# Strassen products for the linear maps of a two-layer graph attention kernel, with their weights' combinations streamed from DRAM

## The chip, the cores and the metric

The kernel runs on one core of a Trainium2 chip. The metric is the device time of one launch in microseconds (us); quoted times are medians of four runs or more, with the lowest and highest beside them (e7_ring6 was run once). The profile shows one execution. In it PE is TensorE (matmul), PEld its weight load, DVE is VectorE, ACT is ScalarE, POOL is GpSimd, and SP issues DMAs; L341 is line 341 of the kernel that the profile belongs to.

## The reference, cut to what matters

```python
# x: (32, 512, 512) float32, adj: (512, 512) int32 of 0 and 1, all weights 512 x 512 float32
def layer0(x):
    mi, mj = x @ Wi.T, x @ Wj.T                  # Wi, Wj: the halves of W (512, 1024)
    a = adj.astype(float32); deg = a.sum(axis=1)
    return deg[None, :, None] * (mi + b) + einsum('ij,bjo->bio', a, mj)

def layer1(h):                                   # 8 heads of 64
    q, k, v = h @ Wq.T + bq, h @ Wk.T + bk, h @ Wv.T + bv
    scores = where(adj == 0, -inf, q k^T / 8)    # by head
    return softmax(scores) v @ Wo.T + bo

x = layernorm(x + layer0(x))
x = layernorm(x + layer1(x))
```

Everything is float32. For one of the 32 batches there are six maps of a 512x512 activation by a 512x512 weight (two of layer 0, then V, Q, K and the output map), beside scores, values, row sums and one aggregation with the adjacency.

## The kernel before: the parts that the change touches

The kernel gives TensorE its work in one order. For batch `b` there are eight steps; each puts two blocks of scores, the values of the step before and, every second step, the row sums ahead of a share of the linear maps of the neighbouring batches. Every map works in 512-column matmuls from resident weights, with two PSUM banks `mm` taken in turn.

```python
def mm_tile():
    return psum.tile([P, 512], FT, name="mm", bufs=2)

def l0_out(b, ic):                               # layer 0, 128 rows of the result
    y = XT[b][:, ic, :]
    nc.vector.scalar_tensor_tensor(y, b0_r, deg_c[:, ic:ic + 1], y, op0=OP.mult, op1=OP.add)
    pm = mm_tile()
    for w, src in ((0, XD[b]), (1, AX_T[b])):
        for dc in range(DC):
            nc.tensor.matmul(pm, src[:, dc, ic * P:(ic + 1) * P], (wi, wj)[w][:, dc, :], ...)
    ...
    nc.vector.tensor_add(y, y, pm)

def q_out(b, hp):                                # ScalarE evicts Q and K
    pm = mm_tile()
    for dc in range(DC):
        nc.tensor.matmul(pm, wq[:, dc, hp * P:(hp + 1) * P], HT[b][:, dc, :], ...)
    nc.scalar.activation(QT[b, hp], pm, AF.Identity, bias=bq_c[:, hp:hp + 1], scale=QSCALE)

def scores(b, hp, kc): ...                       # PE scores, ACT exp, DVE mask product and sum
def invert(b, hp, part): ...                     # reciprocal of the row sums, in halves
def scale(b, hp):
    pl, rl = RL[hp]
    nc.vector.tensor_tensor_reduce(t, pl, rl, 1.0, 0.0, OP.add, OP.add, told[:, j:j + 1])
    OT[b, hp] = work([P, N], "oT", 6)
    nc.vector.tensor_mul(OT[b, hp], PV[hp], rl)  # the scaled head pair, input of the output map

for step in range(STEPS):                        # of a batch; cut
    scores(b, hp, 2 * half); scores(b, hp, 2 * half + 1)
    values(...)                                  # of the step before
    ...
    while at < len(todo) and done < total * (step + 1) / STEPS - 1e-6:
        while extra and todo[at][1] is proj:     # what is left of invert and scale goes first
            g = extra.pop(0); g[0](*g[1:])
        run(todo[at]); done += todo[at][0]; at += 1
        if extra:                                # else one of them after each piece
            g = extra.pop(0); g[0](*g[1:])
```

## Time and profile before

| | before |
|---|---|
| time | 4171.16 us (4170.17 to 4171.29) |
| profiled span, mean granted TensorE clock | 4170.1 us, 0.997 |
| TensorE busy | 4129.6 us, 99% |
| one batch in mid-run ("period") | 128.49 us, no TensorE idle |
| first scores of batch 1 start | 105.8 us |
| first period, which has no output map yet | 113.97 us |
| tail, after the 31st period | 95.5 us |

The page's lines and the rows that this table rests on stand in the prediction. A span is read here as start, then 31 periods from the first scores of batch 1 (each period ends at the first scores of the next of the 32 batches), then the tail after the last of them. A row of "stretches" gives the length of a stretch and then the busy time of PE, weight load, DVE, ACT and POOL, the granted clock, the share of the DMA engines and GB/s.

### The profile page before, as it was taken

To read this page: it belongs to the slowest core of one execution; us is meant where nothing else is said; L and a number is where in the kernel's file an instruction comes from. 1 tells how busy PE (TensorE), PEld (TensorE's weight loads), DVE (VectorE), ACT (ScalarE), POOL (GpSimd) and SP (SyncE) were. 2 spreads that over 40 slices of the span, in tenths; PEclk is the share of its full clock that TensorE was granted. 3 is DMA by queue.
4 is the path that set the end of the run, shared out by engine and by line. 5 is a ranking of instruction groups with operands and counts; after the bars stand their busy time and mean duration, and the time that the engine had idled before them with its cause. 6 is when DMAs were issued, how large, how long until landed. Compare 5 with 4: busy or idle time off the path is not lost.

```text
span 4170.1 us, 31849 instructions
## 1 busy us (share of the span) xinstructions
PE 4129.6 (99%) x12826; PEld 1784.0 (43%) x12826; DVE 2554.7 (61%) x2953; ACT 891.2 (21%) x1159; POOL 566.2 (14%) x782
## 2 busy tenths in 40 slices
PE   8999999999999999999999999999999999999997
PEld 4444444444444444444444444444444444444442
DVE  2566656666557665566565666655766556656567
ACT  1212221222221222212222122221222221222211
POOL 1111111111111111111111111111111111111111
PEclk9999999999999999999999999999999999999999
DMA  3000000000000000000000000000000000000000
GB/s 108 1 21 21 5 16 20 21 20 21 1 20 21 21 21 0 21 21 21 21 0 21 20 21 21 14 7 21 21 21 21 0 21 21 21 21 1 21 10 21
DMA packets 37945, 77.34 MB, mean 19 GB/s; under 512 B 1248, under 2 KB 1248, under 8 KB 37792
## 3 DMA queue, kind: packets, MB, share of 16 engines
q1 hardware_dynamic: 35376, 70.26, 4.7%
q10 hardware_dynamic: 2112, 4.19, 0.3%
q8 instruction: 103, 1.69, 0.2%
q0 software_dynamic: 304, 0.79, 0.1%
q14 instruction: 50, 0.41, 0.0%
HBM read 41.68 MB, written 33.55 MB: 18 GB/s over the span
## 4 chain that ended last, share of the span: by engine, by line
PE 98%; DVE 2%; DMA 0%; ACT 0%; POOL 0%; issue 0%
PE mm L223 21%; PE sc L276 11%; PE ov L293 11%; PE mm L265 11%; PE mm L249 11%; PE mm L257 11%; PE mm L321 11%; PE mm L206 6%; PE ov L300 3%; PE sc L239 2%; PE sc L199 1%; DVE e L280 0%; DVE rl L306 0%; DMA l<-in_adj_dram 0%; DVE es L285 0%; DVE es L283 0%
## 5 line engine op out<-in xcount | busy, mean ns | idle before, releaser
L280 DVE TENSOR_TENSOR e<-e,edge 128x1024 f32<-128x1024 f32 x512 | 710.6, 1408 | 957.0 <-ACT e L279 956.9
L279 ACT ACTIVATE e<-sc 128x1024 f32<-128x1024 f32 x512 | 496.3, 1021 | 1519.3 <-PE sc L276 1519.3
L276 PE MATMUL sc<-q,k 64*128 64x512 f32 x2048 | 510.6, 617 | 0.0
L293 PE MATMUL ov<-e,v 128*64 128x512 f32 x2048 | 496.9, 605 | 6.2 <-DVE e L280 3.7
L265 PE MATMUL mm<-l,wk 128*128 128x512 f32 x1024 | 466.7, 598 | 0.0
L321 PE MATMUL mm<-wo,oT 128*128 128x512 f32 x1024 | 460.0, 602 | 5.6 <-DVE oT L314 5.6
L223 PE MATMUL mm<-wi,l 128*128 128x512 f32 x1024 | 460.6, 592 | 0.0
L257 PE MATMUL mm<-l,wq 128*128 128x512 f32 x1024 | 460.4, 592 | 0.0
L223 PE MATMUL mm<-wj,l 128*128 128x512 f32 x1024 | 460.3, 592 | 0.0
L249 PE MATMUL mm<-wv,l 128*128 128x512 f32 x1024 | 450.3, 592 | 0.0
L306 DVE RECIPROCAL rl<-ov 128x256 f32<-128x256 f32 x256 | 438.2, 1733 | 0.0
L187 POOL TENSOR_TENSOR xlo<-xh,xhi 128x512 fp32r<-128x512 f32 x128 | 165.5, 1301 | 1512.5 <-ACT xhi L186 1512.5
L285 DVE TENSOR_TENSOR es<-es,e 128x1024 f32<-128x1024 f32 x256 | 313.5, 1225 | 8.8
L321 PEld LDWEIGHTS mm<-wo,oT 128*128 128x128 f32 x1024 | 189.8, 190 | 274.0 <-issue 218.0
L276 PEld LDWEIGHTS sc<-q,k 64*128 64x128 f32 x2048 | 176.7, 186 | 304.0 <-issue 293.0
L265 PEld LDWEIGHTS mm<-l,wk 128*128 128x128 f32 x1024 | 189.5, 190 | 265.2 <-issue 215.7
L257 PEld LDWEIGHTS mm<-l,wq 128*128 128x128 f32 x1024 | 194.5, 190 | 245.2 <-issue 245.2
L223 PEld LDWEIGHTS mm<-wj,l 128*128 128x128 f32 x1024 | 194.6, 190 | 244.9 <-issue 244.9
L173 POOL TENSOR_SCALAR mv<-mv 128x1 f32<-128x1 f32 x256 | 71.0, 278 | 1660.4 <-DVE mv L172 1660.4
L227 DVE TENSOR_TENSOR xh<-xh,mm 128x512 f32<-128x512 f32 x128 | 88.0, 688 | 319.0 <-PE mm L223 319.0
L249 PEld LDWEIGHTS mm<-wv,l 128*128 128x128 f32 x1024 | 189.5, 190 | 214.6 <-issue 214.6
L223 PEld LDWEIGHTS mm<-wi,l 128*128 128x128 f32 x1024 | 189.5, 190 | 213.8 <-issue 211.3
(62 smaller groups left out, 2891.7 us busy)
## 6 DMA issues: line engine op xcount, KB each, us to landing
xh<-in_x_dram SPq DMA_DIRECT2D x32, 1024.0 KB, 5.1
out_dram<-xh SPq DMA_DIRECT2D x32, 1024.0 KB, 4.3
wj<-in_wjT_dram ACTq DMA_DIRECT2D x1, 1024.0 KB, 11.9
l<-in_adj_dram SPq DMA_DIRECT2D x1, 1024.0 KB, 9.7
wi<-in_wiT_dram ACTq DMA_DIRECT2D x1, 1024.0 KB, 16.8
wv<-in_wvT_dram SPq DMA_DIRECT2D x1, 1024.0 KB, 20.5
wk<-in_wkT_dram ACTq DMA_DIRECT2D x1, 1024.0 KB, 21.6
wq<-in_wqT_dram SPq DMA_DIRECT2D x1, 1024.0 KB, 25.4
```

The lines of the kernel that those rows point to most:

```text
L206: nc.tensor.matmul(pm, parts[w][:, jc, :], adjR[:, jc, :], start=(w == 0 and jc == 0), stop=(w == 1 and jc == NC - 1))
L223: nc.tensor.matmul(pm, src[:, dc, ic * P:(ic + 1) * P], (wi, wj)[w][:, dc, :], start=(w == 0 and dc == 0), stop=(w == 1 and dc == DC - 1))
L249: nc.tensor.matmul(pm, HT[b][:, dc, ic * P:(ic + 1) * P], wv[:, dc, :], start=(dc == 0), stop=(dc == DC - 1))
L257: nc.tensor.matmul(pm, wq[:, dc, hp * P:(hp + 1) * P], HT[b][:, dc, :], start=(dc == 0), stop=(dc == DC - 1))
L265: nc.tensor.matmul(pm, wk[:, dc, hp * P:(hp + 1) * P], HT[b][:, dc, :], start=(dc == 0), stop=(dc == DC - 1))
L276: nc.tensor.matmul(ps[:, s, :], KT[b, hp][r, kc * P:(kc + 1) * P], QT[b, hp][r, :], start=True, stop=True)
L279: nc.scalar.activation(e, ps, AF.Exp)
L280: nc.vector.tensor_tensor(e, e, edge[:, kc:kc + 1, :].to_broadcast([P, 2, N]), op=OP.mult)
L285: nc.vector.tensor_add(ES[hp], ES[hp], e)
L293: nc.tensor.matmul(PV[hp][s * HD:(s + 1) * HD, :], V[b][:, kc, c0:c0 + HD], E[kc][:, s, :], start=(kc == 0), stop=(kc == NC - 1))
L306: nc.vector.reciprocal(rl[:, c], pl[:, c])
L321: nc.tensor.matmul(pm, OT[b, hp][:, ic * P:(ic + 1) * P], wo[:, hp, :], start=(hp == 0), stop=(hp == HP - 1))
```

## The change

Strassen's scheme (in Winograd's form) makes a 512x512x512 product from seven products of 256x256x256 instead of eight. The intent is to take up to an eighth of the linear maps' time off TensorE, which is the bound (busy for 99% of the span, and 98% of the chain that ended last). The price is additions: of the weights' quarters once, of the activations' quarters for every batch (on POOL), and of the products (on VectorE and POOL). The weights' tiles, seven for each of six maps, are not kept in SBUF: they are written to DRAM at the start and read back for every batch into a ring of 12 tiles. Two maps run at a time, piece by piece in turn, each with one PSUM bank, and pieces that share a result are accumulated in that bank between evictions.

The diff, cut to its core (the cut parts are the fallback path, the start and the small steps of the norm):

```diff
-    def mm_tile():
-        return psum.tile([P, 512], FT, name="mm", bufs=2)
+    def mm_tile(bank):
+        return psum.tile([P, 512], FT, name="mm" + bank, bufs=1)
...
+    RING = 12
+    def combine(name, eng):                      # once per weight
+        a11, a12, a21, a22 = ...
+        eng.tensor_tensor(s1, a21, a22, op=OP.add)        # s2, s3, s4 alike
+        for i, t in ((1, a11), (2, a12), (6, s2), (7, s3), (4, n22), (5, s1), (3, s4)):
+            WS[name, i] = dram.tile([P, 2, Q], FT, ...)
+            nc.sync.dma_start(WS[name, i], t)
+    def prefetch():                              # keeps RING tiles ahead of TensorE
+        while len(TILES) < min(len(KEYS), ring.used + RING):
+            t = ring_tile()
+            nc.sync.dma_start(t, WS[KEYS[len(TILES)]])
...
+    def base(b):                                 # was in l0_out, one 128-row block at a time
+        for ic in range(NC):
+            nc.vector.scalar_tensor_tensor(y, b0_r, deg_c[:, ic:ic + 1], y, ...)
+    def combos(T, b, quarters, which, part=None):  # activations' combinations
+        for i in which:
+            dst, p, q = {1: (t1, b12, b11), 2: (t2, b22, t1), 3: (t3, b22, b12), 4: (t4, t2, b21)}[i]
+            nc.gpsimd.tensor_tensor(dst, p, q, op=OP.subtract)
+    GROUP = {1: "X", 2: "X", 6: "Y", 7: "Y", 4: "Y", 5: "Z", 3: "Z"}
+    def piece(kind, b, i, bank):                 # one of the seven products, 8 or 16 records
+        if first: OPEN[kind, b, g] = mm_tile(bank)
+        ...
+                    nc.tensor.matmul(pm[:, c * Q:(c + 1) * Q], lhs, rhs, start=first, ...)
+        prefetch()
+        if i == 1: nc.scalar.copy(p1, pm)        # product 1 is wanted in every quarter
+        if kind in ("l0", "pj"):                 # layer 0 and the output map add into x
+            if i == 1: three nc.gpsimd.tensor_tensor(d, d, p1, op=OP.add)
+            else:      nc.vector.tensor_tensor(d, d, pm, op=OP.add)
+        elif kind == "v": ...                    # nc.scalar.copy or nc.vector.tensor_tensor
+        else: ...                                # Q and K: two activations for piece 2,
+                                                 # else two nc.vector.scalar_tensor_tensor
...
+    ORDER = (1, 2, 6, 7, 4, 5, 3)
+    def phase_a(n):   # K pieces of n-1 in bank a, between the aggregation of n
+        ...
+            res += k[i:i + 1] + g[i:i + 1]
+            if i == 1 and g:
+                res += [z(combos, TX, n, ..., (1,)), z(combos, TA, n, ..., (1,))]
+        if g: res += [..., z(base, n), ...]
+    def project(m, i):
+        res = [pc("pj", m, i, "b")]
+        if i == 2:
+            res = [FLUSH] + res + [z(combos, TO, m, ot_quarter(m), (2, 3, 4))]
+    def phase_b(n):   # layer 0 of n in bank a, output map of n-2 in bank b, in turn
+        for i in ORDER:
+            res.append(pc("l0", n, i, "a"))
+            ...
+            res += project(m, i)
+    def phase_c(n):   # V in bank a, Q in bank b, the first K pieces
+        res = [norm[0], norm[1], z(apply, n, 1), z(add_bo, n, 0), pc("v", n, 1, "a")]
+        ...
+        res += [pc("q", n, 1, "b"), pc("v", n, 2, "a"), pc("q", n, 2, "b")]
+        ...
+        res += [norm[2], z(combos, TH, n, h, (1, 2), 0), pc("k", n, 1, "a"), norm[3], ...,
+                z(combos, TH, n, h, (3, 4), 1), z(add_bo, n, 1), pc("k", n, 2, "a")]
+        for i in ORDER[2:]:
+            res += [pc("v", n, i, "a"), pc("q", n, i, "b")]
...
-                while extra and todo[at][1] is proj: ...
+                if todo[at] is FLUSH:            # only here the rest of invert and scale goes first
+                    while extra: ...
```

## The prediction

> **What bounds the kernel now.** I read the page's engine shares and chain first, then stretches of one period, then the groups with their shapes, then narrow timelines. In the page's first and fourth parts:
>
> ```profile
> PE 4129.6 (99%) x12826; PEld 1784.0 (43%) x12826; DVE 2554.7 (61%) x2953; ACT 891.2 (21%) x1159; POOL 566.2 (14%) x782
> ...
> PE 98%; DVE 2%; DMA 0%; ACT 0%; POOL 0%; issue 0%
> PE mm L223 21%; PE sc L276 11%; PE ov L293 11%; PE mm L265 11%; PE mm L249 11%; PE mm L257 11%; PE mm L321 11%; PE mm L206 6%; PE ov L300 3%; PE sc L239 2%; PE sc L199 1%; DVE e L280 0%; DVE rl L306 0%; DMA l<-in_adj_dram 0%; DVE es L285 0%
> ```
>
> TensorE is both the busiest engine and the path. The linear maps (L223, L265, L249, L257, L321) are 65% of it. A stretch of one batch in mid-run (columns: length, then busy time of PE, weight load, DVE, ACT, POOL; clock):
>
> ```profile
> 1027.40:1155.89 128.49, 128.49 (x402) 55.50 (x401) 79.59 (x93) 27.66 (x36) 17.36 (x24) 1.00 0.05 17
> ```
>
> A period is 128.49 us with no TensorE hole. The first scores start at 105.83 us; 31 periods bring it to 4089; the tail to 4170 is 81. So time = start + 31 periods + tail.
>
> The pace of one matmul, in the timeline of PE and in the groups:
>
> ```profile
> 2011.73 3.60 PE L257 MATMUL mm<-l,wq 128*128 128x512 f32 x8
> 2015.17 3.60 PE L265 MATMUL mm<-l,wk 128*128 128x512 f32 x8
> ```
>
> The second starts 3.44 us after the first: 8 records, 4 matmuls, so 0.43 us a record (two records a float32 matmul). The groups' mean of 592 ns includes the pipeline's latency and is not the pace.
>
> [...] the trace shows 188 to 190 with latency, which would hide under 216 only just. The last matmul of the kernel settles it:
>
> ```profile
> L410 PE MATMUL mm<-tot,ones 128*128 128x1 f32 x2 | 0.4, 260 | 3.9 <-DVE tot L408 3.9
> L410 PEld LDWEIGHTS mm<-tot,ones 128*128 128x128 f32 x2 | 0.3, 188 | 4.7 <-DVE tot L408 4.7
> ```
>
> Two loads of 188 ns cover only about 0.3 us and two matmuls of 260 ns about 0.4, so a load-and-multiply pair can repeat every 0.13 us or so: loads do not set the pace at 216. [...]
>
> ```profile
> 2135.14 1.23 DVE L280 TENSOR_TENSOR e<-e,edge 128x1024 f32<-128x1024 f32 x1 [10.34 <-ACT e L279]
> ...
> 2149.96 3.33 DVE L280 TENSOR_TENSOR e<-e,edge 128x1024 f32<-128x1024 f32 x2 [9.95 <-ACT e L279]
> 2148.56 2.51 POOL L187 TENSOR_TENSOR xlo<-xh,xhi 128x512 fp32r<-128x512 f32 x2 [43.07 <-ACT xhi L186]
> ```
>
> The mask product costs 1.23 us alone; two take 3.33 rather than 2.4 where POOL was in its subtraction. [...] In the tail, where TensorE stood idle, the stretches show it (seventh number of a row is the clock):
>
> ```profile
> 4081.50:4084.90 3.40, 0.57 (x2) 0.00 (x0) 3.37 (x5) 0.00 (x0) 0.00 (x0) 0.98 0.00 0
> 4084.90:4091.70 6.80, 6.59 (x14) 2.02 (x16) 3.09 (x6) 1.78 (x2) 0.74 (x2) 0.51 0.01 2
> ```
>
> **The change part by part.**
> TensorE, removed: 6 maps x 16 matmuls x 2 records x 429 ns = 82.4 us a period. Added: 6 maps x 7 products x 4 matmuls x 2 records x 216 ns = 72.6. The other 46.1 us (scores, values, sums, transposes, aggregation) stay. Floor of a period: 118.7 us, 9.8 less. A full eighth of 82.4 would be 10.3[...].
>
> VectorE: before 79.6 us a period. Added, with a 128x512 add from PSUM at 0.69 (row L227): two more evictions each for layer 0 and the output map, one for V, and for Q and K, which ACT evicted, two adds and six half-size adds each (about 0.4). That is 5 x 0.69 + 2 x (1.4 + 2.4) = 11 us. Reciprocals are cut in four, about 0.6 more in all. Some 91 to 92 us, 77% of the floor: not the bound on average.
>
> POOL: before 17.4. Added: 16 combinations and 6 adds of 128x512 at 1.3 (row L187): 29 us, so 46[...].
>
> DMA: 42 tiles of 256 KB, 11 MB a period, 93 GB/s, plus x and the output. At the start this trace moved 385 GB/s, and the ring looks 12 tiles, some 20 us, ahead. Hidden.
>
> What is not hidden is order. Each of two PSUM banks now belongs to one piece of 1.73 us, so an eviction must be through before the other bank's piece ends; before, it had 3.4 us or more. I walked one period in the instruction order of the changed kernel, which has eight steps (scores, values, then pieces), with this trace's durations (VectorE operations that do not depend on one another start 0.08 us early):
> - Step 1. The second output piece needs the last head pair's scaled output. VectorE has two reciprocal quarters, the accumulating pass (0.69) and the scaling (0.69) in its queue behind the eviction of the layer-0 piece just before. From the end of that piece: 0.2 signal + 0.6 eviction + 0.83 + 0.94 (quarters, half of the 1.73 of row L306) + 0.62 + 0.69 + 0.1, less the 0.43 of a first matmul that need not wait: **3.5 us** of TensorE idle.
> - Step 4. VectorE arrives 3.0 us late (reciprocal, pass and scaling of the pair before), then has two mask products and two sums (4.8), statistics (1.7) and the eviction of the last output piece (0.7) ahead of the first Q piece: it can start at 10.2 us into the step, and would have at 8.1. **2.0 us**.
> - Step 5: V's third piece waits for a POOL combination made after the transposes, 0.6. Step 6: an eviction behind two products and two sums, 0.6.
> - [...] (POOL's adds against sums in step 4, its combinations against products in step 8): about 1.0, the weakest number[...].
> Sum 7.7 us, so a period of 126.4.
>
> Start: all weights must be combined, 42 tiles stored and read back before the first piece, since stores and ring loads share one queue in order. 9 MB in and 11 MB out at 385 GB/s is 52 us; first piece at about 55 where before it was 35; then layer 0 alone 24, Q, K, V 36, gathers and norms 11, waits 8: first scores at about 135 (before 105.8, but one batch's gather, 9.3, has moved into it from the periods). Tail about 6 longer. Fixed part 135 - 9 + 87 = 213.
>
> Time = 213 + 31 x 126.4 = 4131; I choose 4125.
>
> **Rivals.** (a) The pure TensorE count wins: the walk is too pessimistic, VectorE catches up, no hole: 213 + 31 x 119 = 3900. For it: TensorE bound at 99%, VectorE at 77%. Against: the hole in step 1 is a fixed chain, not a matter of load. With holes of some 4 us: 4013.
> (b) [...]a hole of 3.5 us leaves a window of 3.4 us mostly empty, and in the tail of this trace a window at 0.57 of 3.40 busy was followed by 6.8 us at half clock. If most periods pay 1.7 to 3.4 us: 4190 to 4220.
> (c) [...]with 24 products and normalizations a period each blocked 1 us, VectorE would be near 110 us busy and the period about 130: 4240.
> (d) The ring starves: only if a store of x blocks the queue for over 20 us; a 1 MB store lands in 4.3 here. Unlikely.
>
> **Range and chances.** (a) half true and (b) or (c) half true bound the range: 3990 to 4250. 4088 is the 2% line, which is a period of 125.0, only 1.4 us below my own, and the walk's terms are each uncertain by as much; a hand walk also tends to count holes that overlap. So faster 0.35, same 0.45, slower 0.20.
>
> **What would show each step.** Pieces of 8 records spaced 1.73 us: the floor is right. PE waits on DVE at the output map's pieces totalling about 110 us (31 x 3.5), and at the Q pieces about 60: the walk is right. DVE busy near 92 to 96 us a period, POOL near 46 to 50; mask products' mean far over 1.4 us would speak for (c); a clock below 1.00 in mid-run stretches for (b); PE waits on DMA in mid-run for (d). I would be wrong low if the narrow matmul's pace is above 216 ns, and wrong high if the output pieces do not wait.

The paces in its count can be read in the traces: from the start of one record of a linear map to the start of the next it is mostly 429 ns at 512 columns in the kernel before and 216 ns at 256 columns in the changed kernel. When the count was made no trace had a record of 256 columns, and its 216 was the estimate; half of the 0.43 us of the trace is 0.215. The half clock after a window that TensorE left mostly idle, and the longer products beside POOL's work, stand in the rows that it prints: a clock of 0.51 after 0.57 us busy of 3.40, and 3.33 us for two products of 1.23 us each. The 188 to 190 ns there are the profile's time of one weight load. By what means POOL's work makes VectorE's longer, no trace shows.

## The result, and the profile after

| | before | after |
|---|---|---|
| time | 4171.16 us (4170.17 to 4171.29) | 4300.54 us (4299.13 to 4303.21) |
| profiled span, mean granted clock | 4170.1 us, 0.997 | 4297.4 us, 0.971 |
| first scores of batch 1 | 105.8 us | 141.3 us |
| first period, no output map yet | 113.97 us | 110.27 us |
| period in mid-run, mean of the second to the 30th | 128.49 us | 131.44 us |
| mean of the first 30 periods | 128.01 us | 130.73 us |
| last period | 128.49 us | 124.3 us |
| tail | 95.5 us | 109.8 us |

Two of these stretches of the kernel before, its first period and its tail:

```profile
105.83:219.80 113.97, 112.39 (x357) 48.58 (x357) 65.82 (x71) 27.66 (x36) 13.90 (x16) 1.00 0.00 1
...
4074.58:4170.07 95.49, 72.21 (x223) 24.19 (x222) 72.43 (x88) 16.30 (x17) 11.97 (x16) 0.91 0.06 23
```

The kernel is slower: the ratio of after to before is 1.0311, with a 95% interval of 1.0294 to 1.0329. A ratio is the mean time of one kernel's runs over that of the other's in the same rounds, so it is not quite the ratio of the two medians. The result is numerically correct, as are all the experiments below.

First the page of the changed kernel: the busy times, then the chain that ended last, by engine.

```profile
PE 3967.8 (92%) x17442; PEld 2710.3 (63%) x17442; DVE 3057.1 (71%) x3898; ACT 878.9 (20%) x1230; POOL 1628.2 (38%) x1626
...
PE 71%; DVE 22%; ACT 3%; POOL 2%; issue 1%; SPq 0%; DMA 0%; ACTq 0%; DVEq 0%; POOLq 0%
```

TensorE lost 162 us of busy time and yet the span grew by 127: it is busy for 92% where it was 99%, and the chain now runs through VectorE for 22% where it was 2%. The two kinds of work take turns in waiting for each other.

The 30 periods as one stretch of the changed kernel:

```profile
141.27:4063.27 3922.00, 3681.12 (x16254) 2518.69 (x16253) 2834.17 (x3605) 812.51 (x1139) 1493.93 (x1486) 0.98 0.33 100
```

By 30, a period has 122.70 us of TensorE busy and 8.03 us idle (without the short first period, 123.30 and 8.13); VectorE is busy for 94.5 us, POOL for 49.8. The idle part is in a few rows of PE's waits (the columns are us in total, times, and the longest):

```profile
PE mmb L341 <- DVE oT L437: 103.0, 30, 3.4
PE mma L341 <- DVE k L384: 62.4, 31, 2.1
PE mma L341 <- POOL big L310: 29.3, 30, 1.0
PE ov L414 <- DVE told L432: 28.0, 36, 3.0
...
PE mmb L341 <- DVE xh L359: 12.3, 29, 0.4
...
PE mma L341 <- ACT p L348: 9.8, 31, 0.3
PE mma L341 <- ACT big L287: 7.4, 31, 0.2
```

The number of times, about 30, says that each is a fixed place of the period, not chance. The biggest is the second piece of the output map (bank b, `mmb`) behind the last scaled head pair `oT`. It looks like this in the changed kernel's timelines of PE and of DVE (start, length, engine, line, and in brackets the idle time before and its releaser):

```profile
1970.58 3.62 PE L341 MATMUL mma<-ring,big 128*128 128x256 f32 x16
1974.04 0.59 PE L341 MATMUL mmb<-ring,oT 128*128 128x256 f32 x2
1978.07 2.93 PE L341 MATMUL mmb<-ring,oT 128*128 128x256 f32 x6 [3.43 <-DVE oT L437]
...
1974.31 0.69 DVE L359 TENSOR_TENSOR xh<-xh,mma 128x512 f32<-128x512 f32 x1 [0.29 <-PE mma L341]
1974.91 1.76 DVE L427 RECIPROCAL rl<-ov 128x128 f32<-128x128 f32 x2
...
1977.32 0.69 DVE L437 TENSOR_TENSOR oT<-ov,rl 128x512 f32<-128x512 f32 x1
```

This is the hole that the prediction walked: VectorE evicts the layer-0 piece that ended at 1974.0, and only then finishes the reciprocals, the pass and the scaling. VectorE is not late for that eviction: it waited 0.29 us for TensorE before it. Earlier in its queue lie four base additions, which took 6.30 us from 1961.55.

The six matmuls after the hole take 2.93 us where six at the pace of full clock take 1.5 (an estimate from the pieces below: 6 x 0.216, and 0.16 for the end of the last). Stretches of one window each around that hole and around the second largest wait (first number after the comma: PE busy; seventh: the clock):

```profile
1973.62:1977.03 3.41, 1.01 (x5) 0.56 (x3) 3.08 (x5) 0.00 (x0) 3.41 (x3) 1.00 0.47 154
1977.03:1983.86 6.83, 5.79 (x14) 4.63 (x15) 1.67 (x4) 0.00 (x0) 6.21 (x6) 0.50 0.14 41
2082.84:2086.25 3.41, 1.45 (x7) 0.82 (x5) 3.38 (x5) 0.58 (x1) 0.35 (x1) 1.00 0.24 77
2086.25:2089.66 3.41, 3.29 (x8) 2.66 (x9) 0.67 (x2) 0.00 (x0) 0.00 (x0) 0.50 0.00 0
```

After 3.41 us with TensorE busy for 1.01 the clock is halved for 6.83 us; after a window with 1.45 it is halved for 3.41 us. The clock records of this run hold full and half clock alone, so its mean clock of 0.971 makes 2 x 0.029 x 4297 = 249 us at half clock.

In the clock records of the changed kernel and of the one before, all changes of a run lie on one grid of 3.413 us. Cutting the 30 periods of the changed kernel along it gives 1097 windows at full clock and 51 at half. The 37 of the 1097 that were followed by half clock had TensorE busy, by the profile's count, for 1.49 us or less; the other 1060 had 1.52 or more. Of the 51 at half clock, 37 had at least 2.91 us busy and were followed by full clock; the other 14 had at most 2.38 and were followed by half clock again. This is what these windows show and no rule: in the tail of the kernel before, a window with 3.05 us busy was followed by half clock. In these periods, then, a hole was followed by half clock where it left some 1.9 us (3.41 - 1.49) or more of one window idle, and where the grid fell decided whether it did.

The changed kernel shows what this costs without any edit. Its periods drift against the grid, and two of them, three periods apart, read:

```profile
909.34:1042.63 133.29, 125.16 (x546) 85.72 (x545) 94.92 (x121) 27.10 (x38) 50.17 (x51) 0.96 0.34 99
...
1304.76:1435.00 130.24, 122.11 (x545) 83.58 (x544) 94.93 (x121) 27.10 (x38) 50.16 (x51) 0.99 0.34 101
```

Both have 8.13 us of idle TensorE and the same work, but 10.24 and 3.41 us at half clock, three windows and one: the difference is 3.05 us in TensorE's busy time. In mid-run a period has 6.00 us at half clock on average.

The second wait, in step 8, in the timelines of DVE, POOL and PE:

```profile
2078.43 3.62 DVE L397 TENSOR_TENSOR e<-e,edge 128x1024 f32<-128x1024 f32 x2 [1.12 <-ACT e L396]
2081.97 3.56 DVE L406 TENSOR_TENSOR es<-es,e 128x1024 f32<-128x1024 f32 x2
2085.45 0.87 DVE L384 SCALAR_TENSOR_TENSOR k<-mma,bk_c,p 128x256 f32<-128x256 f32 x2
...
2078.71 4.48 POOL L310 TENSOR_TENSOR big<-big 128x512 f32<-128x512 f32 x2
...
2086.37 3.60 PE L341 MATMUL mma<-big,ring 128*128 128x256 f32 x8 [2.08 <-DVE k L384]
```

VectorE's two products and two sums run beside POOL's two combinations and are long by about 1.1 us for each pair (3.62 and 3.56 us, where e4_combos_dve has 2.54 and 2.47 without them); the eviction of K's piece behind them is late by that, and the next K piece uses the same bank.

At full clock and without a wait, the pieces run as follows:

```profile
2056.30 1.89 PE L341 MATMUL mma<-ring,big 128*128 128x256 f32 x8
2058.03 1.89 PE L341 MATMUL mmb<-big,ring 128*128 128x256 f32 x8
```

They are 1.73 us apart, so 216 ns a record, as predicted.

### The profile page after: what moved, and what is told of

Same layout as the page of the kernel before. It is cut to its first block, busy times and chain, and to the rows that moved or that the text cites. A ratio compares the mean times of both kernels' runs of the same rounds, so it can differ in the third digit from the quotient of the medians.

```text
span 4297.4 us, 46876 instructions
## 1 busy us (share of the span) xinstructions
PE 3967.8 (92%) x17442; PEld 2710.3 (63%) x17442; DVE 3057.1 (71%) x3898; ACT 878.9 (20%) x1230; POOL 1628.2 (38%) x1626
## 3 DMA queue, kind: packets, MB, share of 16 engines
q8 instruction: 142, 2.33, 0.2%
## 4 chain that ended last, share of the span: by engine, by line
PE 71%; DVE 22%; ACT 3%; POOL 2%; issue 1%; SPq 0%; DMA 0%; ACTq 0%; DVEq 0%; POOLq 0%
PE mma L341 32%; PE mmb L341 17%; PE sc L393 8%; PE ov L414 7%; DVE e L397 6%; DVE es L406 6%; PE mmb L265 3%; DVE rl L427 3%; PE ov L421 3%; POOL big L310 2%; DVE ov L432 1%; DVE xh L359 1%; ACT e L396 1%; DVE st L232 1%; DVE oT L437 1%
## 5 line engine op out<-in xcount | busy, mean ns | idle before, releaser
L341 PE MATMUL mma<-ring,big 128*128 128x256 f32 x5296 | 1255.7, 388 | 42.0 <-POOL big L310 29.3
L341 PEld LDWEIGHTS mma<-ring,big 128*128 128x128 f32 x5296 | 1024.0, 195 | 235.6 <-POOL big L310 40.4
L397 DVE TENSOR_TENSOR e<-e,edge 128x1024 f32<-128x1024 f32 x512 | 646.1, 1302 | 236.9 <-ACT e L396 236.8
L310 POOL TENSOR_TENSOR big<-big 128x256 f32<-128x256 f32 (+1 forms) x512 | 603.6, 1202 | 414.6 <-DVE big L259 220.6
L341 PE MATMUL mma<-big,ring 128*128 128x256 f32 x1792 | 446.2, 393 | 74.8 <-DVE k L384 62.4
L427 DVE RECIPROCAL rl<-ov 128x128 f32<-128x128 f32 x512 | 466.7, 933 | 0.0
L341 PE MATMUL mmb<-big,ring 128*128 128x256 f32 x1792 | 438.7, 388 | 16.6 <-DVE xh L359 12.3
L341 PEld LDWEIGHTS mma<-big,ring 128*128 128x128 f32 x1792 | 338.6, 195 | 167.1 <-DVE k L384 76.0
L341 PEld LDWEIGHTS mmb<-big,ring 128*128 128x128 f32 x1792 | 328.2, 190 | 151.2 <-DVE e L397 47.9
L356 POOL TENSOR_TENSOR xh<-xh,p 128x512 f32<-128x512 f32 x192 | 277.7, 1473 | 119.0 <-ACT p L348 118.3
L341 PE MATMUL mmb<-ring,oT 128*128 128x256 f32 x720 | 218.9, 449 | 103.1 <-DVE oT L437 103.0
L341 PE MATMUL mmb<-ring,big 128*128 128x256 f32 x1104 | 269.8, 389 | 12.9 <-POOL big L310 12.9
```

What stands on the lines that cost most here:

```text
L310: nc.gpsimd.tensor_tensor(dst, p, q, op=OP.subtract)
L341: nc.tensor.matmul(pm[:, c * Q:(c + 1) * Q], lhs, rhs, start=first, stop=(kc == 1 and n == len(terms) - 1), skip_group_check=True)
L356: nc.gpsimd.tensor_tensor(d, d, p1, op=OP.add)
L397: nc.vector.tensor_tensor(e, e, edge[:, kc:kc + 1, :].to_broadcast([P, 2, N]), op=OP.mult)
L427: nc.vector.reciprocal(rl[:, c], pl[:, c])
```

## The experiments

Nine kernels were run, each beside the kernel before (4171.2, 4171.0 or 4171.1 us). "Idle" and "busy" are those of TensorE in the 30 periods from the first scores of batch 1, by 30. The first of these periods has no output map and takes 109.4 to 111.2 us in each kernel, so a period in mid-run is longer than this mean by 0.3 to 0.7 us (131.44 us in the changed kernel, 120.63 in e9_stats). The run of e7_ring6 was a single one; the others are medians.

| run | what differs from the changed kernel | time | ratio to before | period | idle | busy | mean clock |
|---|---|---|---|---|---|---|---|
| (changed kernel) | | 4300.5 | 1.0311 | 130.73 | 8.03 | 122.70 | 0.971 |
| e1_fill | idle matmuls fill the hole of step 1 | 4242.1 | 1.0171 | 129.00 | 4.71 | 124.29 | 0.987 |
| e2_flush | scaling one piece earlier in step 1 | 4242.7 | 1.0172 | 128.98 | 7.02 | 121.96 | 0.979 |
| e3_flush_base | e2, and base additions moved | 4152.4 | 0.9955 | 125.78 | 5.29 | 120.49 | 0.989 |
| e4_combos_dve | step 8's combinations moved to VectorE | 4244.1 | 1.0175 | 129.00 | 6.02 | 122.97 | 0.969 |
| e5_all | e3 and e4 | 4076.1 | 0.9777 | 123.38 | 3.29 | 120.09 | 0.992 |
| e6_best | e5, base later still, order of transposes, tail | 4027.5 | 0.9653 | 121.92 | 2.33 | 119.59 | 0.992 |
| e7_ring6 | ring of 6 tiles | 4306.6 | | 130.85 | | | 0.969 |
| e8_bank | e6, order of K, Q and V pieces | 3999.0 | 0.9587 | 120.98 | 1.42 | 119.56 | 0.990 |
| e9_stats | e8, statistics after an eviction | 3982.5 | 0.9547 | 120.31 | 1.01 | 119.30 | 0.990 |

### e1_fill: is it the empty time or the clock behind it?

Theory A: the wait for VectorE is one part, and the half clock that the hole sets off is another, which the prediction's sum left out. Rival B: the clock is halved for another reason, such as the weight loads or the many short matmuls. Matmuls with no use fill the hole without touching any wait or order of VectorE.

```diff
-            res = [FLUSH] + res + [z(combos, TO, m, ot_quarter(m), (2, 3, 4))]
+            res = [FLUSH, z(dummy)] + res + [z(combos, TO, m, ot_quarter(m), (2, 3, 4))]
+    def dummy():                                 # into a scores tile that nothing reads
+        ps = turn_tile()
+        for i in range(4):
+            nc.tensor.matmul(ps, ident, deg_r, start=(i == 0), stop=(i == 3))
```

> Four unused matmuls (8 records, 3.4 us) are put into the hole before the second output piece, into a PSUM tile that nobody reads; nothing else moves. Theory A ([...]which costs some 2.2 us of every period on top of the hole): mid-run clock returns from 0.97 to 1.00, the layer-0 piece after the hole takes 3.45 us again instead of 5.1, and the time falls by about 30 x 2.2 = 66 us, to 4235, although the hole itself is only filled, not removed. Rival B (the clock is halved for another reason, such as the denser weight loads or the many short matmuls): the clock stays at 0.97 and the time stays at 4300, or rises.

Measured: 4242.09 us (4241.02 to 4245.08). TensorE does 3.45 us more work a period (8 records at 0.43), and the kernel is 58 us faster. The row of `oT` is gone from PE's waits; the others are the same to 0.1 us. In the same 30 periods:

```profile
140.10:4010.04 3869.94, 3728.64 (x16485) 2525.48 (x16484) 2834.10 (x3605) 812.50 (x1139) 1494.57 (x1486) 0.99 0.33 102
```

Busy without the added work is 124.29 - 3.45 = 120.84, against 122.70. So the old work itself took 1.86 us less, and the mean clock rose from 0.971 to 0.987 (249 us at half clock became 110). Rival B is out: all weight loads and short matmuls are still there, and adding work to the place where TensorE waits made it faster. What the clock cost behind this one hole is about 1.7 us a period, since the added work replaced the hole one for one and the period still fell by 1.73. The mean clock did not return to 1.00 as expected: about every second period still has one window at half clock, behind the wait of step 8, and takes 130.5 us where those without take 128.8.

### e2_flush and e3_flush_base: what makes the hole?

Theory A, taken alone, has the hole as a matter of order: the scaling waits behind the eviction of a layer-0 piece, so put the scaling ahead of that piece. Theory C: VectorE is already late when step 1 begins, because of the four base additions, which take longer beside POOL's work (1633 ns each in the changed kernel, where a 128x512 operation of POOL ran beside each of the 128; 716 in the kernel before, where none ran beside any), and the order alone gives only part back.

```diff
 for i in ORDER:                                  # phase_b
+    if i == 2:
+        res.append(FLUSH)
     res.append(pc("l0", n, i, "a"))
```

> The remaining reciprocal quarters, the accumulating pass and the scaling are put ahead of the layer-0 eviction in VectorE's queue (flush one piece earlier). Theory A (the hole is only the order of those four operations behind that eviction): it goes from 3.6 us to near nothing, the clock returns to 1.00, time falls by 30 x 5.8 = 174 us to about 4125. Theory C (VectorE also arrives late in that step, held up by the base additions and mask products[...]): the hole only shrinks to about 2.6 us, much of the clock loss stays, time about 4260 to 4275.

Measured: 4242.72 us (4241.41 to 4243.74), a gain of 58 us that lies closer to C, and beyond it. The wait remained, at two thirds of its size:

```profile
PE mmb L341 <- DVE oT L437: 71.6, 30, 2.7
```

In VectorE's timeline of this run the queue ahead of the scaling has no gap from the base additions on (then two products, a sum and four reciprocals of 3.38 us from 2593.72), so now VectorE is late:

```profile
2583.04 6.28 DVE L278 SCALAR_TENSOR_TENSOR xh<-b_r,deg_c,xh 128x512 f32<-128x512 f32 x4
```

Of the 1.75 us that the period fell, 1.05 is in the wait and the rest in busy time (clock 0.979). Two stretches of this run, the second at half clock:

```profile
2595.52:2598.93 3.41, 1.03 (x5) 0.60 (x4) 3.38 (x6) 0.00 (x0) 3.41 (x4) 1.00 0.52 154
2598.93:2602.34 3.41, 3.41 (x10) 2.70 (x9) 0.78 (x2) 0.00 (x0) 3.41 (x4) 0.50 0.04 8
```

The idle time in this window was a single wait of 2.38 us.

Then e3 also moves the base additions, from before step 1 to after the second output piece:

```diff
-                    z(base, n),                       # phase_a
+                    *([z(base, n)] if n < 2 else []),
 res += project(m, i)                             # phase_b
+if i == 2:
+    res.append(z(base, n))
```

> As the flush run, and the four base additions, which take 6.5 us at the end of the step before while they collide with POOL, are moved behind the second output piece. Theory C: VectorE reaches the reciprocals some 5 us sooner, the hole closes to 0.5 us or less, the clock returns to 1.00, time about 4120 to 4140. If the flush alone has closed the hole already, this adds nothing. If the hole stays above 2 us, something other than VectorE's order holds the scaling.

Measured: 4152.36 us (4150.05 to 4152.89): C's direction, 90 us better than e2, but 12 us above the top of what it expected. The row of `oT` is gone. A smaller wait came in its place, the eviction of output piece 6 behind the moved additions in step 2:

```profile
PE mmb L341 <- issue: 17.4, 29, 0.6
```

Theory C is shown for the part that e2 left. In the changed kernel itself the order alone set the hole, since VectorE waited for TensorE before the eviction; its lateness stood behind and showed only when the order was mended. So closing the hole took both moves. How much of the lateness is POOL's work beside the additions and how much their place, e3 does not separate: they still took 1553 ns each. What half clock is left in e3's periods (one window in about every fifth) stands behind the wait of step 8.

### e4_combos_dve: POOL's work beside VectorE's in step 8

Theory D: K's piece in step 8 waits for VectorE because its two mask products and two sums there, 7.2 us in all, take longer beside POOL's two combinations. Rival E: VectorE is simply late, and more work on it makes the kernel slower, by up to 70 us. The edit gives those two combinations to VectorE, one piece later in its queue.

```diff
-            if i == 1 and g:
-                res += [z(combos, TX, n, ..., (1,)), z(combos, TA, n, ..., (1,))]
+            if i == 2 and g:
+                res += [z(combos, TX, n, ..., (1,), None, nc.vector),
+                        z(combos, TA, n, ..., (1,), None, nc.vector)]
```

> The two first combinations of layer 0's inputs move from POOL to an idle stretch of VectorE (1.2 us each); VectorE gets more work, POOL less[...]. Theory D (the wait of the second K piece, 2.2 us a period[...]): these four operations fall from 7.2 to about 4.9 us, the wait goes, time falls by 30 x 2.2 = 66 us to about 4235. Rival E (VectorE is simply short of time): its added 2.4 us per period make the wait longer and the time rises by up to 70 us.

Measured: 4244.05 us (4243.52 to 4244.22), 56 us faster although VectorE has more instructions. The row of `k` (62.4 us) is gone, that of `oT` (103.0) stays. The same place of the period, in DVE's timeline of this run:

```profile
2051.70 2.54 DVE L397 TENSOR_TENSOR e<-e,edge 128x1024 f32<-128x1024 f32 x2 [1.13 <-ACT e L396]
2054.16 2.47 DVE L406 TENSOR_TENSOR es<-es,e 128x1024 f32<-128x1024 f32 x2
...
2057.94 1.28 DVE L310 TENSOR_TENSOR big<-big 128x512 f32<-128x512 f32 x2
```

Products and sums take 2.54 and 2.47 us where they took 3.62 and 3.56, so POOL's combinations beside them cost VectorE 2.2 us. The two combinations that cost POOL 4.48 us cost VectorE 1.28. D is shown and E is out. Busy time did not fall (122.97, clock 0.969): the window behind step 8 is gone, but the period is now mostly 129.70 us, 38 windows of 3.413, so it meets the grid at nearly the same place every time, and there the hole of step 1 costs two windows at half clock in almost every period, 6.71 us where the changed kernel had 6.00.

### e5_all and e6_best: do the repairs add up?

e5 is e3 and e4 in one kernel.

> Both repairs together: flush and base additions (148 us less than the changed kernel when alone) and the first combinations on VectorE (56 us less when alone). If they are separate losses on the path, the gains add: 4300 - 148 - 56 = 4096 us. If they were the same slack counted twice (VectorE's lateness handed from one step to the next), the sum gains less, 4120 to 4150.

Measured: 4076.11 us (4075.17 to 4082.55), 20 us better than the plain sum. The two repairs help each other: the mean clock is 0.992 here, where it was 0.989 and 0.969 with one of them. With both large waits gone, none of its 30 periods has a window at half clock.

e6 starts from e5 and moves the base additions behind output piece 7, so that they delay no eviction of piece 6; puts transposes 2 and 3 ahead of K piece 1; and gives the tail another order.

```diff
-if i == 2:
+if i == 7:
     res.append(z(base, n))
-res += [q1, v2, q2]; res += [norm2, combos, k1, norm3, combos, ..., k2]     # phase_c, in short
+res += [q1, v2];     res += [norm2, combos, norm3, combos, ..., k1, q2, k2]
-ALONE, with FLUSH and the combinations before piece 6                       # the last output map
+FLUSH and the combinations first, then (1,a) (2,a) (6,b) (5,a) (7,b) (3,a) (4,b)
```

> As the run before, and three more waits that its trace shows are moved off the path: base additions one piece later (0.6 us a period), the transposes of the normalized rows ahead of the second Q piece so that POOL's combinations are ready for V's third piece (some 1.3 us with the wait for the first product's copy), and the combinations of the output map ahead of its first piece in the tail (3 to 8 us once). Period 121 to 122 us against a floor of 118.7, time about 4096 - 30 x 1.9 - 5 = 4035 us. If the period stays above 123, the waits only wander.

Measured: 4027.45 us (4023.14 to 4028.95), with a period of 121.92. The base additions, in DVE's groups by shape of this run:

```profile
L278 DVE SCALAR_TENSOR_TENSOR xh<-b_r,deg_c,xh 128x512 f32<-128x512 f32 x128 | 93.9, 795 | 0.0
```

They take 795 ns each, where the changed kernel had 1633 and e3, which had moved them beside other work of POOL, still 1553. The same instruction on the same data takes half the time at its new place. The total is near what was expected, though not for all the reasons given: the new order of the tail gained nothing (107.0 us in e5 and in e6; its waits only have other names), and the wait of V's third piece did not go, even though POOL's combinations now started earlier against it. This called for another look. The end of K piece 2 and the start of V piece 6 in the timelines of PE and ACT of this run:

```profile
2034.34 1.89 PE L341 MATMUL mma<-big,ring 128*128 128x256 f32 x8
2037.20 1.97 PE L341 MATMUL mma<-ring,big 128*128 128x256 f32 x8 [0.97 <-POOL big L310]
...
2036.27 0.84 ACT L381 ACTIVATE k<-mma,bk_c 128x256 f32<-128x256 f32 x2 [0.89 <-PE mma L341]
```

Both pieces write bank a (`mma`). The second starts 0.09 us after ScalarE's eviction of the first ended. The wait of 0.97 is the same here and in the changed kernel although POOL's times differ. The label seemed to be wrong, which e8 was made to test.

### e8_bank and e9_stats: the wait with the wrong name, and one more

Theory F: the wait is ScalarE's eviction, because K piece 2 and V piece 6 stand one behind the other in one bank. Theory G: it is POOL's combination, as the list of waits has it. The edit puts Q piece 2 (the other bank) between the two and lets POOL's work start one piece later, so that the theories point in opposite directions.

```diff
-res += [norm2, combos, norm3, combos, ..., k1, q2, k2]
+res += [k1, norm2, combos, norm3, combos, ..., k2, q2]
```

> e6_best with the order K piece 1, transposes 2 and 3 with their combinations, K piece 2, Q piece 2, then V piece 6 (before: transposes, K1, Q2, K2, V6). In e6_best TensorE waits 0.97 us a period before V piece 6 and the list of waits puts it down to a POOL combination. Theory F: the label is wrong; K piece 2 and V piece 6 stand one behind the other in the same PSUM bank, and the wait is ScalarE's eviction of K piece 2 (two ACTIVATEs, 0.84 us, plus the signals). With Q piece 2 (other bank) between them it goes: the row of 28 us falls to under 6, the period from 121.9 to about 121.1, the time from 4027 to about 4003. Theory G: POOL is the cause; its eight combinations now start one piece (1.7 us) later against V piece 6, so the wait grows to about 2.7 us and the time to about 4078.

Measured: 3999.00 us (3997.82 to 4002.90) and a period of 120.98, against 121.92. The row is gone from the list. F holds, G is out.

e9 then moves the statistics of the second half of layer 0 behind the eviction of the last output piece, for which Q piece 1 waited 0.4 us.

```diff
-if i == 3:
-    res.append(z(stats, n, 1))
 res += project(m, i)
+if i == 3:
+    res.append(z(stats, n, 1))
```

> e8_bank with the statistics of the second half of layer 0 put behind the eviction of the output map's piece 3 instead of ahead of it, so that Q piece 1, which takes the bank of that piece, does not wait for them. Theory: the wait of 0.42 us a period (12.4 us, row xh of the waits) goes, and the time falls by another 12 us, to about 3991 (with theory G about 4066). Rival: the later statistics delay the normalization of the second half and with it transposes 2 and 3 or V piece 1; then the gain is under 5 us or it is a loss.

Measured: 3982.51 us (3980.70 to 3983.72), 16 us less where 12 were expected; the row of `xh` is gone. This is the fastest kernel of the study: 4.5% faster than before and 7.4% faster than the change as it was handed over. Its 30 periods:

```profile
140.34:3749.75 3609.41, 3579.10 (x16253) 2474.60 (x16252) 2728.01 (x3665) 813.06 (x1139) 1355.74 (x1426) 1.00 0.36 109
```

TensorE is idle for 1.01 us a period and its busy time is 119.30. Without the short first period these are 0.90 and 119.73: close to the 118.7 of the prediction's count.

### e7_ring6: does the ring matter?

A rival from the prediction, (d), was that the stream of weights starves. Halving the ring should show it.

```diff
-    RING = 12
+    RING = 6
```

> The changed kernel with a ring of 6 tiles in place of 12. If the ring's depth is ample, as its waits say (3.7 us for a transfer in the whole run), the periods stay within 0.5 us of 130.7 and only the start, where the combinations pass through the same ring, gets some 10 us longer: 4300 to 4320. If transfers are near the path, TensorE's waits for the ring appear in every period and the time goes past 4350.

Measured: 4306.59 us in one run, a period of 130.85 against 130.73. So half the ring costs 0.12 us a period, some 4 us of the run, which is about as much as single runs of one kernel differ here. The stream is hidden.

## Why the prediction was wrong

The prediction's sum has a start, periods, a last period without a gather, and a tail. This is how each came out; measured idle and busy are from the stretches and the table above.

| | predicted | measured | difference in the span |
|---|---|---|---|
| first scores | 135 | 141.3 | +6 |
| first period | 126.4, as the others | 110.3 | -16 |
| 29 periods in mid-run | 126.4 each | 131.44 each | +146 |
| last period, without a gather | 126.4 - 9 = 117.4 | 124.3 | +7 |
| tail | 87 | 109.8 | +23 |
| sum | 4131 | 4297 | +166 |

The difference is in the period in mid-run first. There the sum was 118.7 + 7.7, a floor and holes. Measured, it is about 119.7 + 9.2 + 2.5: a floor, holes and the clock.

- **The step that failed most is the one from the holes to the period, "Sum 7.7 us, so a period of 126.4": it leaves the clock out.** The prediction had half clock as rival (b), had the evidence for it from the tail of the kernel before, and predicted holes of 3.5 and 2.0 us in every period, but added nothing for it. What remains of the measured period, 131.44 - 119.7 - 9.2, is 2.5 us, half of the 5.0 us by which the period was missed. Two other readings agree: 6.00 us at half clock can cost up to 3.0, and e1's periods without a window at half clock take 128.8, 2.6 less. e1 shows about 1.7 of it behind the hole of step 1, by making the kernel faster with useless work.
- **The floor held, within 1 us.** A record takes 216 ns, and the best kernel's TensorE is busy for 119.73 us a period in mid-run. So the gain of some 9 us over the 128.49 of before is real. It was there all along, and was spent elsewhere.
- **The holes were about right as a sum of idle, 8.13 us against 7.7, and that was luck: single ones were missed both ways.** "**3.5 us**" for the second output piece was measured as 3.43, by the chain that the walk has. "**2.0 us**" for the first Q piece was too much: VectorE's and ScalarE's waits in that step (`told`, `xh`, `big`) come to about 1.2. Around each of the seven waits the trace also counts as busy the latency of the last matmul before it (a piece of 8 records lasts 1.89 us at a pace of 1.73), so a hole costs 0.16 us more than its idle time: 8.13 + 7 x 0.16 = 9.2.
- **The term that was mis-sized among the holes is "about 1.0, the weakest number", for POOL's work beside VectorE's in steps 4 and 8.** One such place, step 8 alone, cost TensorE 2.0 us a period (62.4 by 31), and e4 shows it: without the two combinations on POOL, the products and sums there take 5.0 us and not 7.2. Besides, the base additions took 1633 ns each (716 before, 795 at their place in e6), 3.7 us more for four of them than before. In the changed kernel this cost nothing yet, because VectorE still waited for TensorE before the eviction of step 1; e2 and e3 show it as the next limit once the order is mended.
- **Rival (c), VectorE made the bound by longer products, was right in kind and not in size.** VectorE was busy for 94.5 us a period, not "near 110" (its own sum, 24 us on 91 to 92, would be 116), and the mask product's mean was 1302 ns, not far over 1.4 us. Here POOL's work beside VectorE's did not make VectorE the bound; in step 8 it cost TensorE 2.0 us a period because one eviction stood behind it. The mean of the products even fell against the 1408 of before; the means that rose were those of base, 1633, and of the first sum, 1627 (1233 before).
- **Step 5 named the wrong cause.** "V's third piece waits for a POOL combination made after the transposes, 0.6" was found at its place, with 0.97, under POOL's name in the list. e8 shows that it was the eviction of the piece before it in the same bank.
- **The ring** was hidden, as said; PE's only wait for it is 3.7 us, once.
- **The first period and the tail** are in part one slip. The prediction counted 31 full periods in the kernel before, whose first is 14.5 us shorter, and so read its tail as 81 us where it is 95.5. The tail grew by 14.3 us, where 6 were expected. It has a wait of 9.5 us for combinations that nothing hides any more, and a mean clock of 0.83 over 109.8 us, which is 2 x 0.17 x 109.8 = 37 us at half clock (before, 0.91 over 95.5 us, or 17). No experiment took the tail apart: e6's other order left it at e5's 107.0 us, so its cause is argued and not shown.
- **Rival (b) had the clock's cost per period right:** 2.5 us lies in its 1.7 to 3.4. Its times do not quite follow from these (31 periods on 4131 make 4184 to 4236, not 4190 to 4220), and it stood beside the sum, not in it.

The rows of VectorE on which this rests, in the changed kernel's groups by shape (busy us, mean ns of one, then idle before it):

```profile
L397 DVE TENSOR_TENSOR e<-e,edge 128x1024 f32<-128x1024 f32 x512 | 646.1, 1302 | 236.9 <-ACT e L396 236.8
...
L278 DVE SCALAR_TENSOR_TENSOR xh<-b_r,deg_c,xh 128x512 f32<-128x512 f32 x128 | 201.7, 1633 | 0.0
```

What stays open: whether the start (141 us against 106) can be shortened was not tried, and it keeps 35 us of the gain in every version. How much of the tail is clock and how much is order was not separated either.

## What to carry to other kernels

When a change makes the bounding engine's pieces smaller, the slack of every eviction behind them shrinks too (here from the 3.44 us of eight records to 1.73), so the gain is only there after each fixed wait of the period has been ordered away. Here the same arithmetic went from 3% slower to 4.5% faster by order alone and by giving two additions to another engine. When you price a repeated TensorE hole, read the clock in the windows after it as well. Here such a hole cost its length and some 1.7 us for each window at half clock (an estimate, half of 3.41; filling the hole of step 1 in e1 took 1.73 off a period), and in the changed kernel's periods one that left 1.9 us of a 3.41 us window idle was enough. And where the list of waits names an engine, compare the end of the eviction of the bank's last user with the start of the waiting matmul before believing the name: here 0.97 us a period was listed under POOL, and went with the order of banks (e8).
